# Two graph layers on one core: the variance ahead of the products with para, half of the adjacency sums in a later gap, the next x loaded ahead of x1's writes

## The chip, the cores and the metric

The kernel runs on one NeuronCore of a Trainium2 chip, as one launch. The metric is the device time of that launch in microseconds. The engines are named as in the profile: PE is TensorE, DVE is VectorE, ACT is ScalarE, POOL is GpSimd; SP is SyncE, whose queue starts nearly all transfers here. All arithmetic is in float32.

## What is computed

The input x has 16 batches of 1024 nodes with 256 channels; adj is one 1024 x 1024 matrix for all batches. Two layers follow each other, each with a residual and a layer norm:

```python
# layer 0, for each batch
c    = mean(x, axis=channels)
A    = 2 * abs(abs(sigmoid(c[None, :] - c[:, None]) - 0.5) - 0.5)
g    = relu((x.T @ (adj * A_symmetric)) * para)        # 256 x 1024: queries of 4 heads
k, v = split(x @ kv_w)
x1   = layernorm(x + softmax(q @ k.T * scale) @ v)
# layer 1, for each batch
h    = relu(x1 @ w1_loop + adj @ (x1 @ w1_neigh) + b1)
h    = relu(h  @ w2_loop + adj @ (h  @ w2_neigh) + b2)
out  = layernorm(x1 + (x1 + h) / 2)
```

## The kernel before

**Stages.** One loop runs over the batches, and its order is written out by hand: every engine works through its instructions in the order in which the Python code makes them. In iteration b the attention of batch b runs in four units (two head pairs by two halves of the queries). A unit is `scores` (TensorE makes 8 score tiles, ScalarE their exponentials, VectorE their sums) and then `outputs` (products with the values). Between the units, in `gap0`, `gap1` and `gap2`, stands work on other batches: the weights of the queries of batch b + 1, the first graph convolution of batch b - 1 and the second of batch b - 2. After the units comes what I call the transition: the products of the queries of batch b + 1 (`q.step`), `q.end`, which gathers them, the layer norm of batch b (class `BlockedNorm`), and the keys and values of batch b + 1.

**Seven products for eight.** From batch 2 on the queries are made by `FastQueries`, and from iteration 2 on the two products with adj by `Joined`, both with a scheme of seven block products in place of eight. `Joined` needs sums of adj's blocks; `adj_sums` makes them once, in iteration 1, and stores them in device memory, from where each iteration fetches them (`both.fetch`).

**The transition.** In `q.end` of FastQueries (L466 to L485), VectorE adds up the seven products into qT, multiplies qT by para (L483), and ScalarE applies the ReLU (L484). Between the additions stands `norm.sum_squares`. `keys` (L333) makes two tiles of keys, each copied from PSUM by ScalarE (L343); ahead of the last quarter of its matmuls it calls `between`, which is `norm.variance` (L313): a small matmul folds the sums, VectorE scales the result (L315), and GpSimd raises it to the power -0.5 (L317). `norm.scale` (L319) and `norm.spread` (L324) follow: x1 is scaled (L322), transposed, and written to device memory in eight transfers (L330). `values` (L346) makes four tiles in two PSUM banks, each copied out by ScalarE (L355), so that the third can't start until the first is copied.

**Buffers.** Most tiles of 128 x 1024 come from one pool of 23 (`row_tile`); x and x1 in node order share three buffers; keys, queries and values have one each.

**Loads.** `load_x` brings batch b + 1 in node order at the start of iteration b, `load_blocked` brings it in blocks of 32 x 32 in `gap0`. From the first, `means` (L251) takes the node means: ScalarE sums (L255), GpSimd scales (L256), a column is written to device memory as a line (L258) and read back into all partitions as c_row (L260). From the second, `channel_major` (L210) makes the transposed x.

Of the kernel before, what the change touches and what calls it, by code (L numbers as in the profile page):

```python
# [10 lines left out]
F32 = mybir.dt.float32  # L11
# [7 lines left out]
def kernel(  # L19
# [31 lines left out]
    nc = tc.nc  # L51
# [132 lines left out]
    def adj_block(i, j, k, rows01):  # L184
        return of_rows(rows01, k) if (i, j) == (0, 1) else half_adj[i, j][:, k, :]

    def adj_sums(rows01):

        names = (1, 3, 2, 4)
        for h in range(2):  # L190
            w11, w21, w22 = (half_adj[ij][:, 2 * h:2 * h + 2, :] for ij in ((0, 0), (1, 0), (1, 1)))
            w12 = rows01[h].rearrange("p (k n) -> p k n", k=2)
            t = {n: row_tile(f"adjT_{n}_{h}") for n in names}
            v = {n: t[n].rearrange("p (k n) -> p k n", k=2) for n in names}
            nc.vector.tensor_sub(v[1], w12, w11)
            nc.vector.tensor_sub(v[3], w22, w12)
            nc.vector.tensor_sub(v[2], w22, v[1])
            nc.vector.tensor_sub(v[4], w21, v[2])
            for n in names:
                nc.sync.dma_start(out=far_adj[n][h], in_=t[n])  # L200

    def adj_blocked(mt):
        t = row_tile(f"adjB_{mt}")
# [44 lines left out]
    def join(part):  # L248
        nc.vector.tensor_add(part[:, 0, :], part[:, 0, :], part[:, 1, :])

    def means(xb, name):  # L251

        c_col = small.tile([P, NT], F32, tag="c_col", name=f"c_col_{name}", bufs=2)
        for t in range(NT):
            nc.scalar.activation(xb[:, t, :], xb[:, t, :], AF.Identity, accum_out=c_col[:, t:t + 1])  # L255
        nc.gpsimd.tensor_scalar_mul(c_col, c_col, 1.0 / C)  # L256
        line = dram.tile([1, N], F32, tag="line", name=f"line_{name}")
        nc.sync.dma_start(out=line.rearrange("o (t p) -> p (o t)", p=P), in_=c_col)  # L258
        c_row = work.tile([P, N], F32, tag="c_row", name=f"c_row_{name}")
        nc.sync.dma_start(out=c_row, in_=line.to_broadcast([P, N]))  # L260
        return c_row, c_col

    def statistics(mv, xb, ts_, name):
        for t in ts_:
# [136 lines left out]
    class FastQueries(Queries):  # L401
# [64 lines left out]
        def end(self, between):  # L466
            qT = work.tile([P, NC, N], F32, tag="qT", name=f"qT_{self.b}")
            u = row_tile(f"U_{self.b}")
            h0, h1 = ts(0, FB), ts(1, FB)
            p = self.p  # L470
            add = nc.vector.tensor_add
            p1 = row_tile(f"P1_{self.b}")[:, h0]
            nc.scalar.copy(p1, p[1])
            add(u[:, h0], p1, p[6])
            add(qT[:, 0, h0], p1, p[2])
            add(u[:, h1], u[:, h0], p[7])
            add(qT[:, 1, h0], u[:, h1], p[4])
            between()
            add(qT[:, 1, h1], u[:, h1], p[5])
            add(u[:, h0], u[:, h0], p[5])  # L480
            add(qT[:, 0, h1], u[:, h0], p[3])
            for cb in range(NC):
                nc.vector.tensor_mul(qT[:, cb, :], qT[:, cb, :], para_sb[:, cb, :])  # L483
                nc.scalar.activation(qT[:, cb, :], qT[:, cb, :], AF.Relu, scale=QSCALE)  # L484
            return qT  # L485

    class Attention:

# [339 lines left out]
    def run():  # L828
# [50 lines left out]
                turn_adj(range(3))  # L879
        qT = q.end()  # L880
        convs = {}
        for b in range(B):
            more = b + 1 < B
            att = Attention(b, xB, qT, kT, v)
            c1, c2, c3 = (convs.get(b - k) for k in (1, 2, 3))
            both = Joined(c1, c2) if c2 else None
            if c1 and more:
                xb = load_x(b + 1, str(b + 1))
            if c2 and more:
                c2.load_h1()  # L890

            def gap0():
                blocked = load_blocked(b + 1, str(b + 1))
                q.c_row, q.c_col = means(xb, str(b + 1))
                c1.inner()
                att.add(0)
                if both:
                    c2.load_x()
                    both.fetch(2, 3)
                    both.left(nc.gpsimd)  # L900
                ready["xT"] = channel_major(blocked, f"xT_{b + 1}")

            def weigh_first():
# [4 lines left out]
            def gap1():  # L908
                for t in (0, TJ):
                    q.load(t)  # L910
                if both:
                    both.fetch(1, 4)
                    both.run({1: (lambda: q.left(nc.gpsimd),),
                              2: (lambda: att.add(1),),
                              6: (lambda: q.likeness(0), lambda: c3 and c3.moments()),
                              7: (lambda: q.likeness(TJ),),
                              5: (weigh_first,),
                              4: (lambda: c3 and c3.finish(out[b - 3]),),
                              3: (c1.turn_blocks,)})
                else:  # L920
                    q.left(nc.gpsimd)
                    for t in (0, TJ):
                        q.likeness(t)
                    store("01", rows01)
                    c1.first(rows01, lambda: (att.add(1), adj_sums(rows01), weigh_first()))
                    c1.turn_blocks()

            def gap2():
# [7 lines left out]
            for u in range(len(UNITS)):  # L936
                att.scores(u)
                if u == 3 and between:
                    for t in (2, TJ + 2, 3, TJ + 3):
                        q.load(t)  # L940
                    for t in (2, TJ + 2, 3, TJ + 3):
                        q.likeness(t)
                    q.right(1)
                if u and not between:
                    att.add(u - 1)
                att.outputs(u)
                if u == 2 and more:
                    if c1:
                        for t in (1, TJ + 1):
                            q.load(t)  # L950
                            q.likeness(t)
                            q.times_adj(t)
                    else:
                        for t in range(3):
                            q.load(t)
                            q.weigh(t)
                if u < 3 and between:
                    between[u]()
                if u == 0 and more and not between:
                    q.c_row, q.c_col = means(xb, str(b + 1))  # L960
            norm = BlockedNorm(xB, att.sums, str(b))
            if more and not c1:
                xT = ready["xT"]
                for t in range(3, NT):
                    q.load(t)
                for t in range(3, NT):
                    q.likeness(t)
                tiles[3] = adj_blocked(3)
                q.times_adj(3)
                q.step(0)  # L970
                q.times_adj(4)
                q.step(1)
                att.add(3)
                for mt in range(4, NT):
                    tiles[mt] = adj_blocked(mt)
                q.times_adj(5)
                q.step(2)
                q.step(3)
                norm.mean()
                q.times_adj(6)  # L980
                q.times_adj(7)
                q.step(4)
                norm.squares()
                norm.sum_squares()
                q.step(5)
                q.step(6)
                norm.variance()
                xB = load_blocked(b + 1, f"a{b + 1}")
                q.step(7)
                qT = q.end()  # L990
                norm.scale()
                norm.spread()
                turn_adj(range(3, NT))
                kT, v = keys(b + 1, xT), values(b + 1, xT)
            elif more:
                xT = ready["xT"]
                q.pair(2)
                q.step(0)
                q.step(1, lambda: att.add(3))
                q.pair(3)  # L1000
                q.step(2, lambda: (norm.mean(), norm.squares()))
                q.step(3)
                qT = q.end(norm.sum_squares)
                xB = load_blocked(b + 1, f"a{b + 1}")
                kT = keys(b + 1, xT, norm.variance)
                norm.scale()
                norm.spread()
                v = values(b + 1, xT)
            else:
                c2.load_h1()  # L1010
                c2.load_x()
                both.fetch(2, 3)
                c1.inner()
                both.left(nc.gpsimd)
                both.fetch(1, 4)
                both.run({1: (lambda: att.add(3),), 2: (norm.mean, norm.squares, norm.sum_squares), 7: (norm.variance,),
                          5: (norm.scale, norm.spread)})
                c1.turn(0)
                c2.last()
                c1.turn(1)  # L1020
# [33 lines left out]
    with tc.If(count < P):  # L1054
        with tc.For_i(0, B, 1) as b:
            xb = load_x(b, "z")
            xT = channel_major(load_blocked(b, "z"), "xT_z")
            q = Queries("z", xb)
            q.c_row, q.c_col = means(xb, "z")
            kT, v = keys("z", xT), values("z", xT)  # L1060
            for t in range(NT):
                q.load(t)
# [43 lines left out]
```

## Time and profile before

The time before is 2204.62 us, the median of three runs (2204.22 to 2209.49). The profiled execution has a span of 2203.3 us.

| What | us | Where it is read |
|---|---|---|
| score products, s (L508) | 459.4 | costliest groups |
| products with the values, av (L528) | 453.6 | costliest groups |
| sums of probabilities, acc (L517) | 493.3 | costliest groups, VectorE |
| exponentials, pr (L511) | 476.3 | costliest groups, ScalarE |
| the power, rstd (L317), 16 times | 87.1 | costliest groups, GpSimd |
| VectorE's wait for it, ahead of L322 | 84.4 | waits of VectorE |
| VectorE's wait for the blocked x (L214) | 22.1 | waits of VectorE |
| SyncE's queue, x1's writes (L330) behind the scaling (L322) | 360.6 | waits of the SyncE queue |
| SyncE's queue, c_row (L260) behind the line | 120.8 | waits of the SyncE queue |

A group is all instructions of one line, engine and kind of tile, with its time summed. A wait is idle time of an engine just ahead of an instruction, with what ended it. Waits of an engine that isn't the bottleneck cost nothing by themselves, and SyncE's queue is such an engine. In a timeline each row is a start in us, a duration, the engine and line, the operation, and in brackets the idle time before it. A stretch of busy times gives, for each engine, its busy time and the number of instructions.

### The profile page before, as it was taken

The numbers are of one execution on the slowest core, as the hardware profiler recorded it, in microseconds if no ns is written. First come the engines' busy times: TensorE is split into PE (matmuls) and PEld (weight loads), VectorE is DVE, ScalarE is ACT, GpSimd is POOL, SyncE is SP. The second block draws the span as 40 slices with busy tenths as digits, with TensorE's granted clock in tenths as the row PEclk, the third lists the DMA queues.
The fourth block names the chain that finished last, engine by engine and source line by source line (L and its number), as shares of the span: only waits on it lengthen the run. The fifth ranks groups of instructions, "written<-read, shape, count | busy, mean of one in ns | idle before, by whom it ended". The sixth has DMA issues, their size and how long they took to land.

```text
span 2203.3 us, 22846 instructions
## 1 busy us (share of the span) xinstructions
PE 2172.3 (99%) x8082; PEld 1030.9 (47%) x8082; DVE 1806.3 (82%) x2347; ACT 1016.1 (46%) x1304; POOL 334.1 (15%) x192
## 2 busy tenths in 40 slices
PE   9999999999999999999999999999999999999997
PEld 5344444444444444444444445444454444444354
DVE  4978878788887888988889787897878888788965
ACT  4744445544455444445444454535544445534511
POOL 0010020210302103021030301203012030220021
PEclk9999999999999999999999999999999999999999
DMA  9384383552645436355363644627355273553342
GB/s 222 95 117 153 58 190 79 75 184 57 179 106 91 167 60 192 83 105 172 66 182 68 140 138 77 181 58 184 94 87 172 58 191 89 83 176 60 119 134 97
DMA packets 604120, 266.53 MB, mean 121 GB/s; under 512 B 503904, under 2 KB 568288, under 8 KB 604000
## 3 DMA queue, kind: packets, MB, share of 16 engines
q1 hardware_dynamic: 603728, 264.49, 49.7%
q8 instruction: 65, 1.06, 0.2%
q10 hardware_dynamic: 272, 0.52, 0.1%
q14 instruction: 55, 0.45, 0.1%
HBM read 218.76 MB, written 46.20 MB: 120 GB/s over the span
## 4 chain that ended last, share of the span: by engine, by line
PE 61%; DVE 28%; ACT 4%; DMA 2%; issue 2%; SPq 1%; POOL 1%; DVEq 0%; POOLq 0%; ACTq 0%
PE hu_ps L787 15%; PE s L508 14%; PE av L528 14%; DVE acc L517 6%; PE v_ps L353 2%; PE h_ps L694 2%; PE g_ps L391 2%; PE h_ps L695 2%; DVE wg L383 2%; PE t_ps L626 2%; PE hu_ps L633 2%; DVE qT L483 1%; DVE sq_part L310 1%; DVE wg L437 1%; ACT sq L305 1%
## 5 line engine op out<-in xcount | busy, mean ns | idle before, releaser
L511 ACT ACTIVATE pr<-s 128x1024 f32<-128x1024 f32 x512 | 476.3, 1049 | 181.0 <-PE s L508 180.9
L517 DVE TENSOR_TENSOR acc<-acc,pr 128x1024 f32<-128x1024 f32 x384 | 493.3, 1285 | 40.7 <-DVE acc L517 0.5
L508 PE MATMUL s<-qT,kT 64*128 64x512 f32 x2048 | 459.4, 598 | 0.7 <-ACT qT L398 0.7
L528 PE MATMUL av<-pr,v 128*64 128x512 f32 x2048 | 453.6, 595 | 0.0
L508 PEld LDWEIGHTS s<-qT,kT 64*128 64x128 f32 x2048 | 192.1, 187 | 237.4 <-ACT pr L511 112.6
L528 PEld LDWEIGHTS av<-pr,v 128*64 128x64 f32 x2048 | 141.4, 137 | 300.0 <-issue 288.7
L317 POOL TENSOR_TENSOR rstd<-rstd,neg_half 128x32 f32<-128x32 f32 x16 | 87.1, 5444 | 1149.0 <-DVE rstd L315 1149.0
L377 ACT ACTIVATE wg<-c_row,c_col 128x1024 f32<-128x1024 f32 x128 | 147.1, 1149 | 68.5 <-DVE accB L519 48.9
L383 DVE SCALAR_TENSOR_TENSOR wg<-wg,adj 128x1024 f32<-128x1024 f32 x128 | 151.0, 1211 | 20.0 <-ACT wg L378 19.6
L787 PE MATMUL hu_ps<-adj,R 128*128 128x512 f32 x360 | 158.8, 596 | 0.3 <-DMA adj<-adjT 0.2
L378 ACT ACTIVATE wg<-wg 128x1024 f32<-128x1024 f32 x128 | 135.4, 1058 | 4.1
L353 PE MATMUL v_ps<-kvw_sb,xT 128*128 128x256 f32 x512 | 116.9, 382 | 12.1 <-ACT v L355 12.0
L305 ACT ACTIVATE sq<-xB_a 128x1024 f32<-128x1024 f32 x32 | 33.7, 1056 | 192.6 <-DVE xB_a L300 181.1
L464 PE MATMUL g_ps<-wg,S 128*128 128x512 f32 x224 | 116.7, 603 | 0.0
L341 PE MATMUL k_ps<-xT,kvw_sb 128*128 128x512 f32 x256 | 115.8, 597 | 0.0
L464 PE MATMUL g_ps<-T,S 128*128 128x512 f32 x224 | 114.4, 592 | 0.0
L353 PEld LDWEIGHTS v_ps<-kvw_sb,xT 128*128 128x128 f32 x512 | 96.0, 190 | 37.2 <-ACT v L355 17.5
L464 PE MATMUL g_ps<-wg,x 128*128 128x512 f32 x224 | 109.0, 599 | 0.0
L322 DVE TENSOR_TENSOR xB_a<-xB_a,rstd 128x1024 f32<-128x1024 f32 x32 | 38.8, 1255 | 84.4 <-POOL rstd L317 84.4
L787 PE MATMUL hu_ps<-adjT,t 128*128 128x512 f32 x240 | 105.7, 592 | 0.0
L787 PEld LDWEIGHTS hu_ps<-adj,R 128*128 128x128 f32 x360 | 67.1, 190 | 79.9 <-issue 77.5
L515 DVE TENSOR_TENSOR acc<-pr,pr 128x1024 f32<-128x1024 f32 x64 | 77.5, 1211 | 23.8 <-ACT pr L511 23.8
(163 smaller groups left out, 2727.9 us busy)
## 6 DMA issues: line engine op xcount, KB each, us to landing
adj<-in_adj_dram SPq DMA_DIRECT2D x128, 512.0 KB, 4.5
adj<-adjT SPq DMA_DIRECT2D x120, 512.0 KB, 10.2
xB_a<-in_x_dram SPq DMA_DIRECT2D x128, 128.0 KB, 4.0
x1d<-xB_a SPq DMA_DIRECT2D x128, 128.0 KB, 3.4
x<-x1d SPq DMA_DIRECT2D x16, 1024.0 KB, 9.1
xB<-in_x_dram SPq DMA_DIRECT2D x120, 128.0 KB, 4.7
x<-in_x_dram SPq DMA_DIRECT2D x15, 1024.0 KB, 7.1
out_dram<-x SPq DMA_DIRECT2D x15, 1024.0 KB, 4.5
```

What stands on the lines that cost most here:

```text
L317: nc.gpsimd.tensor_tensor(self.rstd, self.rstd, neg_half, ALU.pow)
L341: nc.tensor.matmul(pk[:, ts(j, FB)], kvw_sb[:, cc, ts(kb, P)], xT[:, cc, ts(j, FB)], start=(cc == 0), stop=(cc == NC - 1))
L353: nc.tensor.matmul(pv[:, ts(i, C)], xT[:, cc, ts(g * per + i, P)], kvw_sb[:, cc, C:2 * C], start=(cc == 0), stop=(cc == NC - 1))
L377: nc.scalar.activation(wg, self.c_row, AF.Abs, bias=self.c_col[:, t:t + 1], scale=-1.0)
L378: nc.scalar.activation(wg, wg, AF.Tanh, scale=-0.5)
L383: nc.vector.scalar_tensor_tensor(wg, wg, 1.0, self.adj.pop(t), op0=ALU.add, op1=ALU.mult)
L464: nc.tensor.matmul(self.p[n], x_n[:, k, :], w_n, start=(k == 0), stop=(k == TJ - 1))
L508: nc.tensor.matmul(ps[:, ts(s, FB)], self.kT[rows, pair, ts(mt, P)], self.qT[rows, pair, ts(j, FB)], start=True, stop=True)
L511: nc.scalar.activation(pr, ps, AF.Exp)
L517: nc.vector.tensor_add(acc, acc, pr)
L528: nc.tensor.matmul(pav[s * HD:(s + 1) * HD, :], self.v[:, mt, pair * P + s * HD:pair * P + (s + 1) * HD], self.pr[mt][:, ts(s, FB)], start ...
L787: nc.tensor.matmul(dst, self.x[n][:, k, :], half_adj[w][:, k, :] if w else of_rows(rows, k), start=(start and k == 0), stop=(k == TJ - 1), ...
```

## The change

The change moves work and adds none. There are four edits:

- **Variance first.** `q.end` no longer multiplies by para. That and the ReLU are a method of their own, `scale`, and it's called in the gap of the keys, behind `norm.variance`. So GpSimd's power can run while VectorE multiplies, and the first copy of keys stands ahead of the ReLUs in ScalarE's order.
- **Half of the adjacency sums later.** `adj_sums` makes one half at a call. The first half stays in iteration 1's `gap1`, the second stands in that iteration's transition, behind the keys and ahead of the scaling. One of the two tiles of adj's upper right block is kept until then.
- **The next x early.** `load_x` and `load_blocked` of batch b + 2 are issued in the transition of iteration b, ahead of the writes of x1. Before, they were issued in iteration b + 1, behind them.
- **c_row later in the queue.** `means` is split in two: the load of c_row is issued at the end of `gap0`, so that the load of x1 and the fetches of sums need not stand behind it while it waits for the line.

```diff
-    def adj_sums(rows01):
+    def adj_sums(rows01, h):
         names = (1, 3, 2, 4)
-        for h in range(2):
...
-    def means(xb, name):
+    def means(q, xb, name):
...
+        q.c_col = c_col
+        def row():
+            q.c_row = work.tile([P, N], F32, tag="c_row", name=f"c_row_{name}")
+            nc.sync.dma_start(out=q.c_row, in_=line.to_broadcast([P, N]))
+        return row
...
             add(qT[:, 0, h1], u[:, h0], p[3])
+            self.qT = qT
+            return qT
+
+        def scale(self):
             for cb in range(NC):
-                nc.vector.tensor_mul(qT[:, cb, :], qT[:, cb, :], para_sb[:, cb, :])
-                nc.scalar.activation(qT[:, cb, :], qT[:, cb, :], AF.Relu, scale=QSCALE)
-            return qT
+                nc.vector.tensor_mul(self.qT[:, cb, :], self.qT[:, cb, :], para_sb[:, cb, :])
+                nc.scalar.activation(self.qT[:, cb, :], self.qT[:, cb, :], AF.Relu, scale=QSCALE)
...
             if c1 and more:
-                xb = load_x(b + 1, str(b + 1))
+                xb, blocked = coming
...
+            def load_next():
+                nonlocal coming
+                if b + 2 < B:
+                    coming = load_x(b + 2, str(b + 2)), load_blocked(b + 2, str(b + 2))
...
             def gap0():
-                blocked = load_blocked(b + 1, str(b + 1))
-                q.c_row, q.c_col = means(xb, str(b + 1))
+                row = means(q, xb, str(b + 1))
                 c1.inner()
                 att.add(0)
                 if both:
                     c2.load_x()
                     both.fetch(2, 3)
                     both.left(nc.gpsimd)
+                row()
...
-                    c1.first(rows01, lambda: (att.add(1), adj_sums(rows01), weigh_first()))
+                    c1.first(rows01, lambda: (att.add(1), adj_sums(rows01, 0), weigh_first()))
...
                 qT = q.end(norm.sum_squares)
                 xB = load_blocked(b + 1, f"a{b + 1}")
-                kT = keys(b + 1, xT, norm.variance)
+                load_next()
+                kT = keys(b + 1, xT, lambda: (norm.variance(), q.scale()))
+                if not c2:
+                    adj_sums(rows01, 1)
                 norm.scale()
                 norm.spread()
                 v = values(b + 1, xT)
```

In iteration 0, whose queries are made without the scheme, `load_next` stands behind `q.end` in the same way.

More of the change, by code (lines that the diff above doesn't have):

```diff
@@ L185, in adj_block @@
         return of_rows(rows01, k) if (i, j) == (0, 1) else half_adj[i, j][:, k, :]
-    def adj_sums(rows01):
+    def adj_sums(rows01, h):
         names = (1, 3, 2, 4)
-        for h in range(2):
[L191 to L200, printed above, removed]
+        w11, w21, w22 = (half_adj[ij][:, 2 * h:2 * h + 2, :] for ij in ((0, 0), (1, 0), (1, 1)))
+        w12 = rows01[h].rearrange("p (k n) -> p k n", k=2)
+        t = {n: row_tile(f"adjT_{n}_{h}") for n in names}
+        v = {n: t[n].rearrange("p (k n) -> p k n", k=2) for n in names}
+        nc.vector.tensor_sub(v[1], w12, w11)
+        nc.vector.tensor_sub(v[3], w22, w12)
+        nc.vector.tensor_sub(v[2], w22, v[1])
+        nc.vector.tensor_sub(v[4], w21, v[2])
+        for n in names:
+            nc.sync.dma_start(out=far_adj[n][h], in_=t[n])
     def adj_blocked(mt):
@@ L258, in means @@
         nc.sync.dma_start(out=line.rearrange("o (t p) -> p (o t)", p=P), in_=c_col)
-        c_row = work.tile([P, N], F32, tag="c_row", name=f"c_row_{name}")
-        nc.sync.dma_start(out=c_row, in_=line.to_broadcast([P, N]))
-        return c_row, c_col
+        q.c_col = c_col
[3 more added lines that the diff above has]
+        return row
     def statistics(mv, xb, ts_, name):
@@ L881, in run @@
         convs = {}
+        coming = None
         for b in range(B):
@@ L959, in run @@
                 if u == 0 and more and not between:
-                    q.c_row, q.c_col = means(xb, str(b + 1))
+                    means(q, xb, str(b + 1))()
             norm = BlockedNorm(xB, att.sums, str(b))
@@ L1004, in run @@
                 xB = load_blocked(b + 1, f"a{b + 1}")
-                kT = keys(b + 1, xT, norm.variance)
+                load_next()
+                kT = keys(b + 1, xT, lambda: (norm.variance(), q.scale()))
+                if not c2:
+                    adj_sums(rows01, 1)
                 norm.scale()
@@ L1058 @@
             q = Queries("z", xb)
-            q.c_row, q.c_col = means(xb, "z")
+            means(q, xb, "z")()
             kT, v = keys("z", xT), values("z", xT)
```

## The prediction

> **What bounds the kernel now.** I read the busy shares first. TensorE leaves about 31 us of the span, so no rearrangement can be worth more than that, apart from time in which it is busy at half rate.
>
> ```profile
> PE 2172.3 (99%) x8082; PEld 1030.9 (47%) x8082; DVE 1806.3 (82%) x2347; ACT 1016.1 (46%) x1304; POOL 334.1 (15%) x192
> ```
>
> Then the list of waits for TensorE alone (total us, times, longest), to see whose work it stands for:
>
> ```profile
> PE v_ps L353 <- ACT v L355: 12.0, 13, 1.0
> PE den_ps L540 <- DVE den_part L521: 4.7, 2, 3.8
> PE hu_ps L787 <- DMA adj<-adjT: 0.2, 1, 0.2
> ```
>
> So 12.0 us is one wait that recurs: the third value product needs the bank that the first one used, and ScalarE's copy out of it (L355) is late. It happens in 13 of the 14 transitions of FastQueries. The timeline of the transition at 937 to 955 us shows why, engine by engine:
>
> ```profile
> 942.26 0.30 PE L245 MATMUL sum_ps<-sq_part,fold 128*128 128x32 f32 x2
> 948.74 3.72 PE L353 MATMUL v_ps<-kvw_sb,xT 128*128 128x256 f32 x16 [0.93 <-ACT v L355]
> ...
> 942.94 2.36 DVE L483 TENSOR_TENSOR qT<-qT,para_sb 128x1024 f32<-128x1024 f32 x2
> 945.21 0.18 DVE L315 TENSOR_SCALAR rstd<-sum_ps 128x32 f32<-128x32 f32 x1
> 950.95 2.36 DVE L322 TENSOR_TENSOR xB_a<-xB_a,rstd 128x1024 f32<-128x1024 f32 x2 [5.55 <-POOL rstd L317]
> ...
> 944.19 2.19 ACT L484 ACTIVATE qT<-qT 128x1024 f32<-128x1024 f32 x2 [8.40 <-DVE qT L483]
> 946.29 1.91 ACT L343 COPY kT<-k_ps 128x1024 f32<-128x1024 f32 x2
> 948.09 1.09 ACT L355 COPY v<-v_ps 128x512 f32<-128x512 f32 x2
> ```
>
> ScalarE sits idle for 8.40 us until VectorE's product with para arrives. Behind its two ReLUs stand two copies of keys, the first of which could have been made at about 941 us, and only then the copy that TensorE waits for. That copy ends at 948.09 + 0.59 = 948.68; TensorE goes on at 948.74.
>
> The other wait is in iteration 1, where VectorE makes the adjacency sums (L195 to L198) in one block of eight, from 191.67 to 201.00 us. TensorE's timeline, then its busy time in stretches (the clock is the number behind the POOL column):
>
> ```profile
> 218.84 0.64 PE L540 MATMUL den_ps<-den_part,fold 128*128 128x32 f32 x2 [3.83 <-DVE den_part L521]
> 219.40 9.43 PE L508 MATMUL s<-qT,kT 64*128 64x512 f32 x32
> ...
> 218.00:225.00 7.00, 6.16 (x18) 3.06 (x20) 6.89 (x12) 2.46 (x3) 0.00 (x0) 0.57 0.46 129
> ```
>
> Everywhere else 32 score products take 7.14 us; here 9.43, at a granted clock of 0.57. The pause of 3.83 us so costs a further 2.29.
>
> **What the Trainium skill says.** "TensorE: Matmul & The Clock Gate", part 1 (the HAM clock gate), puts the array at half rate after about 3.4 us of idleness; 3.83 us did so here and the 0.93 us pauses did not. The same page, at the engine queue depths, says that ScalarE and VectorE take instructions strictly first in, first out; the ready copy of keys standing behind the ReLUs agrees. "SBUF — State Buffer", section "Who interferes with whom", says that a VectorE instruction with two SBUF inputs and a GpSimd instruction that reads SBUF exclude each other for a whole instruction. That matters because the change puts the multiplications beside GpSimd's power. The trace is divided: beside the addition of L821, L437 takes 1.64 us instead of 0.68, but beside the power of L272 two such instructions hardly suffer (VectorE, then GpSimd):
>
> ```profile
> 1273.23 2.55 DVE L383 SCALAR_TENSOR_TENSOR wg<-wg,adj 128x1024 f32<-128x1024 f32 x2
> ...
> 1273.40 2.58 POOL L272 TENSOR_TENSOR rstd_g<-rstd_g,neg_half 128x8 f32<-128x8 f32 x1 [6.53 <-DVE rstd_g L271]
> ```
>
> Undisturbed, the pair takes 2.32 to 2.36 us (at 1028.14 us, for one) and the power 1.65 (at 2143.56).
>
> **The change part by part.** No instruction is added or removed; three groups move.
>
> *Variance ahead of the para products, in the keys' gap.* VectorE reaches L315 at 942.9, when the fold (ending 942.56) is there, so nothing waits. L315 delays the multiplications by one issue step, 0.11 us (as between L249 at 940.79 and the addition at 940.90). On ScalarE the first copy of keys now stands ahead of the ReLUs, in time that was idle: 0.90 us (946.29 to 948.09 is two copies) leaves the path. GpSimd's 5.4 us run beside the multiplications instead of after them. How much that slows them is the open size: 0 if the power takes no hold, 0.19 (2.55 - 2.36) if it acts as at 1273 us, 5.44 if it holds the interface throughout. The value copy comes earlier by 0.90 - 0.11 = 0.79 us at best, 0.60 with 0.19; I take 0.70. Of each 0.93 us wait about 0.23 is left: 13 x 0.70 = 9.1 us (7.8 to 10.3; 12.0 if the wait vanishes). VectorE also saves about 2.3 us ahead of L322, which no one waits for: the additions at 955.54 follow without idleness, but the scores bind them.
>
> *Half of the sums moved to the transition of iteration 1.* Four instructions, 191.67 to 196.34, so 4.67 us, leave the block. VectorE would then be ready for the sums of probabilities at 207.09 - 4.67 = 202.4, before its data: the second probability tile ends 1.97 us after ScalarE starts, at 204.0. From that start the chain to den_part takes 13.7 us in a full iteration (953.57 to 967.28), so den_part ends at 202.03 + 13.7 = 215.7, where TensorE is free at 215.0. About 0.8 of the 3.83 us remains, too short for the clock to drop: 3.0 + 2.3 = 5.3 us. The four come back after the multiplications of the transition, about 267.6 to 272.3, in the 5.58 us in which VectorE waited for GpSimd; L322 began there at 273.12 and can again. Queued behind them are only that scaling and the transposes of x1. I cost them at nothing.
>
> *Loads of the next x and its blocked form ahead of x1's writes, c_row behind the fetches.* These were late:
>
> ```profile
> 952.21 6.34 SPq L330 DMA_DIRECT2D x1d<-xB_a  x8
> 958.59 0.78 SPq L96 DMA_DIRECT2D x<-in_x_dram  x1
> 960.47 12.51 SPq L108 DMA_DIRECT2D xB<-in_x_dram  x8
> ```
>
> The writes wait for the scaling, so all behind them wait too. The new place is at about 929 us, when DMA is idle (0 GB/s from 932 to 952). The tiles they take are last used by query products of step 1 and a product with adj of pair 2, both over by 925 us, and the x buffer's former owner was written out at 876. They will land by 942, so nothing queued behind, the x1 writes first of all, is held. ScalarE's sums of x lose a 6.43 us wait; the line then goes out at 964 instead of 973, and c_row, behind five loads, lands near 980, needed at 998. Almost all of this is off the path. What it can give is read from the periods between first scores: 274.54 to 2035.14 is 1760.6 us for 13, against 13 x 135.24 = 1758.1; 2.5 us of excess. In iteration 4, 0.92 of it is a den_ps wait behind a blocked transpose that waited 4.07 us for its load, and 0.21 in iteration 3 is a late fetch. I count these and half of the rest: 1.8 us.
>
> Sum: 9.1 + 5.3 + 1.8 = 16.2 us, so 2204.6 - 16.2 = 2188.4.
>
> **The rivals.** (B) The wait changes its place: the reordered ScalarE queue or the tiles held longer (two more of 23 from the transition to the first gap) stop something else for as long. For it: TensorE's slack in a transition is under 1 us, and the last key copy still stands ahead of the values. Against: no tile that I traced is released late. Then only the sums help: 2204.6 - 5.3 = 2199.3. (C) The power excludes the second multiplication for 5.44 us. The value copy then comes at 948.7 - 0.8 + 5.4 = 953.3, 4.6 us later than before, 14 x 4.6 = 65; such pauses are over 3.4 us and would cost 2.3 us of half rate each, 32 more: 2204.6 + 65 + 32 - 5 = 2297. For it stands L437's 1.64 us; against it the pair at 1273 us.
>
> **How the numbers follow.** My forecast 0.84, B 0.10, C 0.06. All waits gone gives 12.0 + 6.1 + 2.5 = 20.6, so 2184; the weak end of my forecast (7.8, half of iteration 1's gain, nothing from loads) is 10.4, so 2194. I widen this to 2183 to 2197 for sizes I cannot see. Faster by 0.3% means under 2198.0: 0.85; within: 0.08 (B mostly); slower: 0.07.
>
> **What would show it.** In TensorE's waits: v_ps on ACT v at 2 to 4 us in total or gone, and den_ps on den_part under 2. In the transition: keys copied before the ReLUs, L322's idle time before it under 3.5 us, the multiplication pair at 2.4 to 2.6. Iteration 1's third scores at 7.1 us. The period between scores 134.5. DVE's wait for xB (22.1 us over ten) gone. I am wrong if the pair of multiplications takes over 3.3 us, or if a new TensorE wait over 0.5 us recurs.

## The result and the profile after

The changed kernel takes 2187.51 us, the median of four runs (2187.24 to 2187.59), against 2204.69 us (2204.22 to 2209.49, four runs) for the kernel before. The ratio is 0.9917, with a 95% interval of 0.990 to 0.9934. The forecast was 2188.4 us, in a range from 2183 to 2197.

The same reading order as before, now on the kernel after. Busy time of the engines, from the page:

```profile
PE 2168.6 (99%) x8082; PEld 1029.9 (47%) x8082; DVE 1801.7 (82%) x2347; ACT 1016.2 (46%) x1304; POOL 350.8 (16%) x192
```

GpSimd is busy for 16.7 us more (334.1 before), with the same 192 instructions: something on it has grown. TensorE's waits (total us, times, longest):

```profile
PE v_ps L356 <- ACT v L358: 0.8, 2, 0.4
PE den_ps L546 <- DVE den_part L527: 0.8, 1, 0.8
```

The 12.0 us for the value products are down to 0.8, the 4.7 for den_part to 0.8, and the wait for a fetch of adj is gone. The timeline of the transition that the prediction showed (TensorE, VectorE, ScalarE, GpSimd):

```profile
933.60 7.39 PE L356 MATMUL v_ps<-kvw_sb,xT 128*128 128x256 f32 x32
...
931.61 0.69 DVE L484 TENSOR_TENSOR qT<-U,g_ps 128x512 f32<-128x512 f32 x1
932.21 0.18 DVE L318 TENSOR_SCALAR rstd<-sum_ps 128x32 f32<-128x32 f32 x1
932.33 2.42 DVE L490 TENSOR_TENSOR qT<-qT,para_sb 128x1024 f32<-128x1024 f32 x2
938.88 2.36 DVE L325 TENSOR_TENSOR xB_a<-xB_a,rstd 128x1024 f32<-128x1024 f32 x2 [4.14 <-POOL rstd L320]
...
930.14 1.01 ACT L346 COPY kT<-k_ps 128x1024 f32<-128x1024 f32 x1 [4.96 <-PE k_ps L344]
933.59 2.25 ACT L491 ACTIVATE qT<-qT 128x1024 f32<-128x1024 f32 x2 [2.43 <-DVE qT L490]
935.74 0.99 ACT L346 COPY kT<-k_ps 128x1024 f32<-128x1024 f32 x1
936.63 1.21 ACT L358 COPY v<-v_ps 128x512 f32<-128x512 f32 x2
...
932.48 6.37 POOL L320 TENSOR_TENSOR rstd<-rstd,neg_half 128x32 f32<-128x32 f32 x1 [72.11 <-DVE rstd L318]
```

Read ScalarE first. Its idle time of 8.40 us ahead of the ReLUs is split in two, 4.96 and 2.43, with the first copy of keys between them; only one copy of keys is left between the ReLUs and the copy of the values. TensorE's 32 value products run through in one row, with no pause. Counted from the first key product (937.11 before, 926.51 after), the copy of the values starts at +10.98 before and at +10.12 after, 0.86 us earlier, while the products with para start at +5.83 and +5.82: the small scaling of the variance in front of them costs nothing. GpSimd's power takes 6.37 us instead of 5.44; over all its 16 times the power takes 100.2 us instead of 87.1, most of the 16.7.

In iteration 1, the third scores in TensorE's timeline:

```profile
215.77 0.41 PE L546 MATMUL den_ps<-den_part,fold 128*128 128x32 f32 x2 [0.78 <-DVE den_part L527]
216.11 7.14 PE L514 MATMUL s<-qT,kT 64*128 64x512 f32 x32
```

and the stretch of busy times that showed the slow clock before (the clock is the number behind the POOL column):

```profile
218.00:225.00 7.00, 7.00 (x36) 2.73 (x34) 6.68 (x11) 6.72 (x8) 0.00 (x0) 1.00 0.23 77
```

The pause is 0.78 us, the clock stays at 1.00, and the scores take 7.14 us. SyncE's queue, around the same transition:

```profile
922.43 6.98 SPq L108 DMA_DIRECT2D xB<-in_x_dram  x6
940.14 6.25 SPq L333 DMA_DIRECT2D x1d<-xB_a  x8
```

The blocked next x (these are the last six of its eight transfers) goes out some 18 us ahead of x1's writes, and VectorE's list of waits has no line for xB any more (22.1 us before).

Where the time went, read from the starts of each iteration's first scores in the two profiles: iteration 1 is 5.50 us shorter (123.35 to 117.85); iterations 2 to 14 together 12.93 us shorter (1760.60 to 1747.67), most of them now 134.38 us long instead of 135.24. What follows them is 0.6 us longer, so that the span falls by 17.8 us.

### The profile page after: what moved, and what is told of

It is laid out like the page before. It is cut to its first block, busy times and chain, and to the rows that moved or that the text cites. A ratio compares the mean times of both kernels' runs of the same rounds, so it can differ in the third digit from the quotient of the medians.

```text
span 2185.5 us, 22862 instructions
## 1 busy us (share of the span) xinstructions
PE 2168.6 (99%) x8082; PEld 1029.9 (47%) x8082; DVE 1801.7 (82%) x2347; ACT 1016.2 (46%) x1304; POOL 350.8 (16%) x192
## 4 chain that ended last, share of the span: by engine, by line
PE 69%; DVE 24%; ACT 4%; issue 2%; DMA 0%; DVEq 0%; SPq 0%; POOLq 0%; ACTq 0%; POOL 0%
PE s L514 17%; PE hu_ps L793 17%; PE av L534 16%; DVE acc L523 4%; PE v_ps L356 3%; PE t_ps L632 3%; PE h_ps L700 2%; PE hu_ps L639 2%; PE g_ps L394 2%; PE h_ps L701 2%; DVE wg L386 2%; DVE qT L490 1%; DVE sq_part L313 1%; ACT sq L308 1%; DVE wg L440 1%
## 5 line engine op out<-in xcount | busy, mean ns | idle before, releaser
L320 POOL TENSOR_TENSOR rstd<-rstd,neg_half 128x32 f32<-128x32 f32 x16 | 100.2, 6260 | 1110.7 <-DVE rstd L318 1110.7
L325 DVE TENSOR_TENSOR xB_a<-xB_a,rstd 128x1024 f32<-128x1024 f32 x32 | 38.8, 1254 | 60.5 <-POOL rstd L320 60.5
```

What stands on the lines that cost most here:

```text
L320: nc.gpsimd.tensor_tensor(self.rstd, self.rstd, neg_half, ALU.pow)
```

## The experiments

Each kernel was timed beside runs of the kernel before on the same chip. There the kernel before had medians of 2207 to 2212 us, with single runs from 2203 to 2221, so the first results are given as a time and as the difference within the set. The later ones are compared with the changed kernel, whose medians in two sets were 2187.51 and 2187.46.

### Each part alone

**The first part alone**, on the kernel before:

```diff
             add(qT[:, 0, h1], u[:, h0], p[3])
+            self.qT = qT
+            return qT
+
+        def scale(self):
             for cb in range(NC):
...
-                kT = keys(b + 1, xT, norm.variance)
+                kT = keys(b + 1, xT, lambda: (norm.variance(), q.scale()))
```

> The kernel before with the first edit alone: product with para and ReLUs moved into the gap of the keys, behind the variance. The theory (the waits for the value copy were 12.0 us, and the first copy of keys was 0.90 us of each) expects the v_ps waits at 0.8 us or less in total and a time of 2193.5 (11.2 less than 2204.7). The rival (the earlier loads are what lets the transition run through) expects v_ps waits of 6 us or more and a time of 2198 to 2205.

Measured: 2197.42 us (2193.64 to 2201.97), beside 2210.62 for the kernel before: 13.2 us less, ratio 0.9941 (0.9925 to 0.9958). No wait for the value products is left, and the undisturbed iterations take 134.37 us, 0.87 less. The time itself is 3.9 us above the expected figure. The trace shows another wait:

```profile
PE den_ps L543 <- DVE den_part L524: 9.2, 7, 3.8
```

(This is the line of its list of waits for TensorE.) One of the seven is iteration 1's, 3.8 us; the other six, 5.4 us in all, lie in iterations 2 to 5 and 9 and 10. Ahead of the longest of these, 2.17 us, VectorE sat idle for 5.34 us in front of a transpose of the blocked x; for this one the trace names no releaser, but nine others, 24.2 us in all, it puts down to the load. This kernel has the old place of the loads. The profiled run took 2199.16 us, 5.7 above the expectation, which is about the 5.4 of the six waits.

**The sums alone**, on the kernel before:

```diff
-    c1.first(rows01, lambda: (att.add(1), adj_sums(rows01), weigh_first()))
+    c1.first(rows01, lambda: (att.add(1), adj_sums(rows01, 0), weigh_first()))
...
                 kT = keys(b + 1, xT, norm.variance)
+                if not c2:
+                    adj_sums(rows01, 1)
```

> The kernel before with half of the adjacency sums moved into iteration 1's transition, and nothing else. The theory (3.05 us of pause and 2.29 us of half clock) expects 5.3 less, 2199.4, the third scores of iteration 1 at 7.14 us and a den_ps wait of 0.8. The rival (the moved half, here without the multiplications ahead of it, delays the scaling and the scores of iteration 2) expects 2 or more of the 5.3 to come back as a wait in iteration 2: 2201 to 2204.

Measured: 2206.49 us (2202.67 to 2212.96), 4.1 us less, ratio 0.9985 (0.9975 to 0.9996). The time is 7.1 us above the expected figure, the difference 1.2 us below it. In its trace iteration 1 takes 118.69 us, 4.7 less than in the profile of the kernel before. The pause there is 0.78 us and the clock stays up, as expected; but TensorE, now earlier, meets a wait of 0.73 us for the value products in that transition, which it hadn't had. The first part takes that away too, so together they give the 5.50. What the profiled run (2209.16 us) has in excess lies in the later iterations, which have the old place of the loads: in iteration 4, VectorE stands 6.85 us in front of a transpose of the blocked x, TensorE pauses 3.68 us for den_part, and the iteration takes 140.88 us.

**The loads alone**, both early loads and c_row's new place on the kernel before (of its edits, the one in the transition):

```diff
                 xB = load_blocked(b + 1, f"a{b + 1}")
+                load_next()
                 kT = keys(b + 1, xT, norm.variance)
```

> The kernel before with the early loads of the next x and the later c_row, and nothing else. The theory (only the irregular periods, 2.5 us in sum, can be won) expects 1.7 less, 2203.0, all periods from iteration 2 at 135.24 and no v_ps wait shortened. The rival (the loads carry a large part of the gain) expects 2190 to 2199.

Measured: 2203.25 us (2203.05 to 2204.89 in nine runs), 7.4 us less, ratio 0.9968 (0.9956 to 0.9981). The absolute time is the one expected. The difference isn't, since the kernel before took longer on this chip than in the runs that the prediction was made from. With the loads moved, the spread of single runs falls from 12.7 us to 1.8. Its waits for the value products are untouched, 12.5 us over 13.

The three differences add up to 24.7 us; a kernel with all three, the next one, is 24.1 us below the same runs of the kernel before. So the parts add up within the scatter, which is wide: by its interval the first is worth 9 to 17 us, the second 1 to 6, the third 4 to 10.

### Which of the two reorderings in the transition pays

The first part does two things: the power runs beside the products, and a copy of keys leaves ScalarE's path. Two kernels separate them. In the first, the order within the gap is turned round:

```diff
-    kT = keys(b + 1, xT, lambda: (norm.variance(), q.scale()))
+    kT = keys(b + 1, xT, lambda: (q.scale(), norm.variance()))
```

> The changed kernel with the product with para ahead of the variance in the gap of the keys, so that GpSimd's power again runs after the multiplications, while the first copy of keys stays ahead of the ReLUs. The theory (the key copy leaving the path is the gain) expects the time of the changed kernel, 2187.5 within 1, and the wait of L325 for the power back at 5.5 us. The rival (the power running beside the multiplications is the gain) expects the 11.2 us back: 2198.7.

Measured: 2186.55 us (2186.34 to 2186.85), an iteration of 134.31 us. The timelines of VectorE and GpSimd, in the same transition:

```profile
931.22 0.69 DVE L484 TENSOR_TENSOR qT<-U,g_ps 128x512 f32<-128x512 f32 x1
931.94 2.36 DVE L490 TENSOR_TENSOR qT<-qT,para_sb 128x1024 f32<-128x1024 f32 x2
939.95 2.36 DVE L325 TENSOR_TENSOR xB_a<-xB_a,rstd 128x1024 f32<-128x1024 f32 x2 [5.55 <-POOL rstd L320]
...
934.48 5.44 POOL L320 TENSOR_TENSOR rstd<-rstd,neg_half 128x32 f32<-128x32 f32 x1 [74.49 <-DVE rstd L318]
```

Without any overlap of power and products, all of the gain is there. The products take 2.36 us again and the power 5.44, and VectorE's wait ahead of the scaling is 5.55 us, as in the kernel before. Nobody misses it.

In the second, the copy of keys goes back behind the ReLUs, and the overlap stays:

```diff
...
                     between()
+                    if late:
+                        nc.scalar.copy(kT[:, 0, :], first)
...
-            nc.scalar.copy(kT[:, kb, :], pk)
+            first = pk if kb == 0 else first
+            if kb or not late:
+                nc.scalar.copy(kT[:, kb, :], pk)
...
-                kT = keys(b + 1, xT, lambda: (norm.variance(), q.scale()))
+                kT = keys(b + 1, xT, lambda: (norm.variance(), q.scale()), late=True)
```

> The changed kernel, in which the first copy of the keys stands behind the two ReLUs again, so that ScalarE's order is that of the kernel before while VectorE and GpSimd keep the new one (power beside the products with para). Theory: the gain of the first part is the 0.9 us copy that left ScalarE's path, not the power's overlap; so the wait of the third value product comes back in 13 or 14 transitions at 0.85 to 0.95 us each, and the time is 2187.5 + 12 = 2199 us (2198 to 2201). Rival (the overlap of power and products is the gain): the waits stay under 1 us in all and the time is 2187.5 us.

Measured: 2199.99 us (2199.72 to 2200.61), 12.5 us above the changed kernel. Its timeline (ScalarE, then TensorE) has the old picture again:

```profile
940.09 0.99 ACT L344 COPY kT<-k_ps 128x1024 f32<-128x1024 f32 x1
940.98 1.02 ACT L350 COPY kT<-k_ps 128x1024 f32<-128x1024 f32 x1
941.88 1.09 ACT L362 COPY v<-v_ps 128x512 f32<-128x512 f32 x2
...
942.54 3.72 PE L360 MATMUL v_ps<-kvw_sb,xT 128*128 128x256 f32 x16 [0.96 <-ACT v L362]
```

Two copies in a row stand ahead of the values, and the wait is 0.96 us, 14 times, 14.0 us in all. So the gain of the first part is the place of one 0.9 us copy in ScalarE's order; the overlap with the power gives nothing and costs some 0.07 us an iteration.

### Does GpSimd hold VectorE's products off

The prediction left open whether GpSimd's power excludes the products with para. The pair took 2.42 us beside it, so it doesn't hold them for its whole time. Whether a plain GpSimd operation in that place would have, this kernel asks; it adds one to the work:

```diff
+            nc.gpsimd.tensor_mul(by_node(self.sq[0])[:, :, 0:16], by_node(self.xB[0])[:, :, 0:16],
+                                 self.rstd.unsqueeze(2).to_broadcast([P, NB, 16]))
             nc.gpsimd.tensor_tensor(self.rstd, self.rstd, neg_half, ALU.pow)
```

> The changed kernel with one GpSimd product of 128x512 added ahead of the power, in a tile that nobody reads afterwards; it starts with the products with para. It adds work and leaves none out. Theory of exclusion (a plain GpSimd tensor operation holds VectorE's two-input products off, the power does not): the two products take 3.5 to 3.8 us instead of 2.42, the copy of the values comes 1.1 to 1.4 us later, the third value product waits about 1.2 us in each of 14 transitions, and the time is 2187.5 + 17 = 2204 us (2200 to 2207). Rival (no hold at all between the two engines): the pair stays at 2.4 to 2.6 us and the time at 2187.5 to 2189 us; only the scaling behind the power starts 1 to 2 us later, in VectorE's idle time.

Measured: 2199.48 us (2199.28 to 2199.69), 12.0 us above the changed kernel, just under the expected range. Its timeline (VectorE, GpSimd, ScalarE, TensorE):

```profile
936.26 3.22 DVE L492 TENSOR_TENSOR qT<-qT,para_sb 128x1024 f32<-128x1024 f32 x2
936.47 1.93 POOL L320 TENSOR_TENSOR sq<-xB_a,rstd 128x512 f32<-128x512 f32 x1 [72.17 <-DVE rstd L318]
939.51 1.06 ACT L493 ACTIVATE qT<-qT 128x1024 f32<-128x1024 f32 x1 [0.94 <-DVE qT L492]
942.01 3.72 PE L358 MATMUL v_ps<-kvw_sb,xT 128*128 128x256 f32 x16 [0.86 <-ACT v L360]
```

The pair takes 3.22 us: by the records the first product is as short as ever, 1.23, and the second takes 2.08 instead of 1.27. ScalarE then waits 0.94 us between its two ReLUs, and TensorE 0.86 us. I had put the hold at 1.1 to 1.4 us; it is 0.80. The GpSimd operation began 0.21 us behind the first product, so part of its 1.93 us is probably its own waiting for that product. The Trainium skill, in "SBUF — State Buffer", section "Who interferes with whom", says that a VectorE instruction with two SBUF inputs contends with a GpSimd instruction that reads SBUF; the 3.22 us agree.

The power fits that on one side. When it begins beside a product with para, it grows by about what that product still has to run: in the changed kernel by 0.93 us with 1.07 left (932.48 to 933.55), in this kernel, where its row at 938.48 us takes 6.30, by 0.86 with 1.00 left (938.48 to 939.48), and with the order turned round, where no product is running, by nothing. So it seems to wait for the product in flight. The other way there is hardly any hold: the second product, which starts in the middle of the power, takes 1.27 us, 0.05 longer than the first. The power's duration is not time in which VectorE is kept out.

### Would the transition have held both halves of the sums

```diff
-    c1.first(rows01, lambda: (att.add(1), adj_sums(rows01, 0), weigh_first()))
+    c1.first(rows01, lambda: (att.add(1), weigh_first()))
...
                 if not c2:
+                    adj_sums(rows01, 0)
                     adj_sums(rows01, 1)
```

> The changed kernel with the other half of the adjacency sums moved to the transition of iteration 1 as well. Theory (the space there holds one half): the block of iteration 1 loses another 4.7 us, so its remaining wait of 0.78 us for den_part goes; in the transition the scaling of x1 starts about 4.7 us later, the sums of probabilities with it, and TensorE waits 1 to 4 us for den_part in iteration 2, the longer end with a slower clock behind it. Time 2188 to 2193 us. Rival (the transition has room for both): the 0.78 us go and nothing comes back, 2186.7 us.

Measured: 2189.05 us (2188.87 to 2189.38), 1.5 us slower than the changed kernel. The time is in the range expected, but half of the reason was wrong. From the timelines of this kernel, TensorE's and VectorE's:

```profile
288.45 0.41 PE L546 MATMUL den_ps<-den_part,fold 128*128 128x32 f32 x2 [1.45 <-DVE den_part L527]
...
272.15 2.35 DVE L325 TENSOR_TENSOR xB_a<-xB_a,rstd 128x1024 f32<-128x1024 f32 x2
```

The scaling starts 4.73 us later (267.42 in the changed kernel), and 1.45 of it arrives at TensorE: VectorE's chain had about 3.3 us to spare there. But the 0.78 us of iteration 1 did not go. VectorE, even in the changed kernel, sits idle there ahead of its sums of probabilities:

```profile
203.98 1.23 DVE L521 TENSOR_TENSOR acc<-pr,pr 128x1024 f32<-128x1024 f32 x1 [1.07 <-ACT pr L517]
```

With one half moved, it is ScalarE's exponentials that bound this chain, as the prediction had reckoned and as I had forgotten when I wrote the expectation. The second half has nothing left to give.

### Which of the transfers matters

Four kernels take apart the third part, all from the changed kernel. First, the blocked form late again:

```diff
-                xb, blocked = coming
+                xb = coming
...
-                    coming = load_x(b + 2, str(b + 2)), load_blocked(b + 2, str(b + 2))
+                    coming = load_x(b + 2, str(b + 2))
...
             def gap0():
+                blocked = load_blocked(b + 1, str(b + 1))
```

> The changed kernel with the load of the blocked next x issued in the first gap again, ahead of the means but behind x1's writes; the load of x itself stays early and c_row stays behind the fetches. Theory (the blocked form is the transfer whose lateness reaches TensorE: VectorE's transpose of it stands ahead of the sums of probabilities): VectorE's wait for xB comes back in several iterations, a den_ps or hu_ps wait of 0.3 to 2 us with it in some of them, single runs differ by some us, and the time is 2188 to 2193 us. Rival (the load of x, by ScalarE's means, is what mattered, or with x out of the way the blocked form lands in time): 2187.5 us, and runs within 1 us of each other.

Measured: 2187.10 us (2186.66 to 2187.28). The rival was right: VectorE's waits for xB come to 1.0 us, and TensorE has no wait for den_part or adj beyond those of the changed kernel. Then c_row ahead of the fetches again, and, in a kernel of its own, x itself late again; with them the changed kernel once more:

```diff
-                row = means(q, xb, str(b + 1))
+                means(q, xb, str(b + 1))()
...
-                row()
```

> The changed kernel with c_row issued directly behind the line again, ahead of the reads of x1 and of the adjacency sums for pair (2, 3); both loads of the next x stay early. The queue then stands still until the line has landed (about 10 us from 954), and the fetches go out about 10 us later than in the changed kernel. If c_row's place is part of what the loads gave: waits of TensorE for adj of 0.2 to 0.6 us in some iterations, 2188 to 2191 us, single runs some us apart. If only the early x is: 2187.5 us, within 1 us of each other, since with x out of the way the fetches still land by when they are read.

```diff
-                xb, blocked = coming
+                blocked = coming
+                xb = load_x(b + 1, str(b + 1))
...
-                    coming = load_x(b + 2, str(b + 2)), load_blocked(b + 2, str(b + 2))
+                    coming = load_blocked(b + 2, str(b + 2))
```

> The changed kernel with the load of the next x behind x1's writes again; its blocked form stays early and c_row stays behind the fetches. If the 1 MB of x ahead of the blocked form was what made that form late, then here nothing of VectorE waits for a load, and only ScalarE's sums of x wait, about 6 us in each iteration, which nobody on the path needs: 2187.5 to 2188.5 us, runs within 1 us. If ScalarE's wait for x is itself on the path (its copies of t and of snap stand behind those sums): 2189 to 2195 us, with waits of TensorE on ScalarE's copies.

> The changed kernel itself, for runs that share the chip with the two others and with the kernel before: 2187.5 us within 1 us, while single runs of the kernel before lie 5 to 12 us apart.

Measured: 2187.71 us (2187.48 to 2188.13), 2187.51 us (2187.35 to 2187.56), and 2187.46 us (2187.32 to 2187.62) for the changed kernel, with the kernel before at 2208.06. With both loads early, c_row's place gives nothing that can be measured, though the queue does stand still for the line, 139.6 us in all. With x late ScalarE waits 58.2 us for it, in 13 pieces, and TensorE for none of them. So each load alone may go back. Last, both of them:

```diff
-                xb, blocked = coming
+                xb = load_x(b + 1, str(b + 1))
...
-                load_next()
...
             def gap0():
+                blocked = load_blocked(b + 1, str(b + 1))
```

> The changed kernel with both loads of the next x where the kernel before had them, behind x1's writes; of the third part only c_row's place behind the fetches is left. If it takes one of the two loads out of the way to get the blocked form in time (each was enough alone), VectorE's waits for xB come back (about 22 us over ten), with waits of TensorE for den_part or adj of 0.2 to 2 us, runs lie some us apart, and the time is 2189 to 2196 us. If c_row's place alone had been enough: 2187.5 us, runs within 1 us.

Measured: 2195.75 us (2191.88 to 2198.55), 8.2 us above the changed kernel. The waits for xB are back, 23.1 us over nine. The worst of them, from the timelines of VectorE and TensorE:

```profile
567.85 1.25 DVE L213 STREAM_TRANSPOSE xT<-xB 128x1024 f32<-128x1024 f32 x1 [6.06 <-DMA xB<-in_x_dram]
...
582.53 0.41 PE L546 MATMUL den_ps<-den_part,fold 128*128 128x32 f32 x2 [2.90 <-DVE den_part L527]
```

and the stretches of busy times around it, with the clock again behind the POOL column:

```profile
580.00:585.00 5.00, 2.47 (x5) 1.20 (x6) 4.92 (x9) 0.00 (x0) 2.45 (x2) 0.80 1.00 400
585.00:590.00 5.00, 5.00 (x11) 2.20 (x10) 4.76 (x14) 1.82 (x3) 0.04 (x1) 0.85 0.27 109
```

VectorE stands 6.06 us in front of a transpose whose data hasn't landed. Behind it in VectorE's order are the sums of probabilities, so den_part is late; TensorE pauses 2.90 us and then runs at a reduced clock. That iteration takes 139.23 us instead of 134.38. Either load out of the way is enough. What reaches TensorE is the lateness of the blocked form, by way of VectorE, and behind x1's writes that form is late, but for 1.0 us in all, only with the 1 MB of x ahead of it. With both loads late, c_row's place was not tried by itself.

## Why the prediction was right

- **The bound and the wait.** That the value products waited for a copy stuck behind the ReLUs was the right reading: putting the one copy back behind the ReLUs costs 12.5 us, and taking the overlap away costs nothing.
- **The size of the first part: 9.1 us forecast, 11.2 measured.** The mis-sized term is the time charged against the copy's 0.90 us. I took 0.20 off, for an issue step of 0.11 and a slower pair of products. But VectorE starts a product that reads the result of the addition just ahead of it 0.72 us after that addition's start (931.22 to 931.94 in the kernel with the order turned round), and an unrelated instruction after 0.60 (931.61 to 932.21 in the changed kernel). The scaling of the variance fits into that step of 0.12 us, and the products start at the same point as before. The pair is slower by 0.06, not 0.19. So 0.86 us an iteration is gained, and with it practically the whole wait.
- **The power beside the products.** I gave the exclusion of rival C 0.06, and it did not come. VectorE does wait 4.14 us ahead of the scaling of x1 (L322 before, L325 now), not "under 3.5": I had not allowed for the power growing to 6.37 us. The growth stood in the lines at 1273 us that the prediction showed: there the smaller power takes 2.58 us instead of 1.65, 0.93 more, as here. I read them only for what VectorE lost. The growth is off the path: with the order turned round the wait is 5.55 us, and the kernel is 1 us faster.
- **The sums.** 3.0 + 2.3 us forecast, 5.50 measured for iteration 1, and about 0.8 left of the pause, as forecast. Of the 5.50 the sums alone bring 4.7: the forecast left out that TensorE, once earlier, would wait for the value products in that transition too, and the first part spares it this. The 2.3 for the slow clock is one sample: after the same pause of 3.82 us the third scores took 9.85 us in the kernel with the first part alone and 8.83 in the one with the loads alone, 2.7 and 1.7 more than 7.14. The four subtractions in the transition cost nothing: L325 starts with no idle time behind them, and moving all eight there shows some 3.3 us of room beyond the four.
- **The loads: 1.8 us forecast, 1.7 between the two profiles** (12.93 less the 11.2). But this size belongs to the runs that I had seen. On other chips the same part is worth 7.4 us (on the kernel before) and 8.2 us (on the changed kernel), because the kernel before has no fixed time there. The queue of SyncE, which I had called one whose waits cost nothing by themselves, costs this much by what stands behind the waiting writes. I had seen the evidence, a 4.07 us wait of a transpose and 0.92 us of it at TensorE in one iteration, and read it as a small constant. It is a chance of being late, in most iterations, which VectorE's order hands on to TensorE.
- **The sum.** That 16.2 us came so near the 17.2 measured is in part luck. The changed kernel took 2187.5 us in both its sets, but the kernel before did not repeat its time: where the two ran again side by side they lay 20.6 us apart (2208.06 and 2187.46). The time of the changed kernel was forecast well; the size of the gain depends on how late the loads of the kernel before happen to be.
- **c_row.** I listed its earlier fetches under the gains; with the loads early they gave nothing that the runs can show.
- **Rival B** (the wait only changes its place) is refuted by the list of waits: no new wait of TensorE over 0.5 us recurs. Two waits of 0.41 us for the value products remain, in iterations 11 and 13, where VectorE comes to the products with para 0.35 us later.

## What to carry to other kernels

When an engine waits for a copy, look at what stands ahead of that copy in its engine's order, and move ready work in front of the item that isn't ready; here a 0.9 us copy gave 11 us, and the more striking overlap beside it gave nothing. A load that lands just in time in one profile is a spread of run times, not a number: look at how far the runs lie apart, and issue it ahead of any transfer that waits for computing. Before moving the rest of some work off a stage, check that the stage's chain isn't already waiting for data.

## What was unexpected of the hardware

- The length of a pause does not settle whether the clock drops, nor for how long. After a pause of 3.83 us the clock was at half for 6.83 us in the kernel before, after one of 3.82 for 3.41 us in the kernel with the loads alone; a pause of 2.90 us between products (both loads late; 3.73 between the weight loads around it) also brought 3.41 us of it, and one of 2.17 (first part alone) none. In each trace the changes of the clock lie whole multiples of 3.413 us apart: 6.83 is two of them, the 211.63 us at full clock ahead of the drop in the kernel before are 62. So I divided the traces into stretches of that length, set by each trace's own changes. First the stretch ahead of the drop in the kernel before, then one of the two that share the pause of 2.17 us, the one with less work (the number behind the length is TensorE's busy time, the one behind POOL's column the clock):

```profile
213.82:217.24 3.42, 1.19 (x6) 0.14 (x2) 3.28 (x3) 0.00 (x0) 0.00 (x0) 1.00 0.39 159
...
313.82:317.23 3.41, 2.25 (x6) 0.70 (x4) 3.34 (x3) 0.00 (x0) 0.75 (x1) 1.00 1.02 406
```

  In the traces of these kernels there are five drops that a pause brought. TensorE was busy for 0.35 to 1.25 us in the stretch ahead of each, and for 1.76 us or more in every other stretch at full clock from 60 to 2140 us. What lies between the two was not measured, and the ends of matmuls are modelled. The Trainium skill, in "TensorE: Matmul & The Clock Gate", part 1, puts the half rate after an idle window of about 3.4 us. The length of the window agrees; but it need not be idle throughout, and a pause between products that is shorter can be enough.
- GpSimd's power of 128x32 does not hold VectorE's two-input products off, whereas a plain 128x512 product does (2.42 against 3.22 us for the pair). It is the power that gives way, 5.44 to 6.37 us, by about what the product in flight still had to run.
- With both loads behind x1's writes (the kernel before, the first and second parts alone, both loads late), single runs on one chip lie 5 to 14 us apart; with at least one of the loads moved, within 2 us on every chip, 0.1% of the time. So the lateness of these transfers differs from run to run. Why it does is open, and each kernel has a trace of one run only.
